# Single-head f1 rows, pair sums in buffers of their own, and half of a weight product moved, in a four-layer GNN kernel

## The chip, the cores and the metric

The kernel runs on one core of a Trainium2 chip. The time is the device time of one execution in microseconds (us). Engines are named as in the profile: PE is TensorE (matmuls; PEld its weight loads), DVE is VectorE, ACT is ScalarE, POOL is GpSimd, SP is SyncE. [...]

## The reference, cut to what matters

A stack of four graph layers on N = 2708 nodes with F = 512 features; each is followed by a residual sum and a layer norm. Only layer 0 (an attention autoencoder with H = 4 heads of D = 128) and the weights of layer 3 are touched by the change:

```python
# layer 0
Xw  = einsum('hnd,hde->hne', Xh, W)
f1  = einsum('hnd,hd->hn', Xw, V[:, 0, :, 0]);  f2 = einsum('hnd,hd->hn', Xw, V[:, 1, :, 0])
sig = sigmoid(f1[:, :, None] + f2[:, None, :])
att = masked_softmax(adj[None] * sig, adj != 0)         # both patterns are adj
Xc  = einsum('hij,hjd->hid', att, Xw)  ->  n x F
Xn  = batchnorm(Xc)
emb = batchnorm(elu(Xn @ Wm.T + bm) + Xn)               # encoder MLP
Y   = einsum('hij,hjd->hid', att, emb by heads)
Yc  = elu(einsum('hnd,hed->hne', Y, W))
out = batchnorm(elu(Yc @ Wd.T + bd) + Yc)               # decoder MLP
x   = layernorm(x + out)
# layer 3
a = (x @ Wq + bq) @ (x @ Wk + bk).T * scale + adj + adj;  x = layernorm(x + softmax(a) @ (x @ Wv + bv))
```

Layer 1 multiplies by the adjacency divided by its column degrees, layer 2 is an edge softmax over all nodes.

## The kernel before

Nodes are cut into 22 blocks of 128 rows (the last has 20); the 2708 columns of the attention matrix into two halves `hf` of HW = 1354; the heads into two pairs `p`. What decides the order of instructions on each engine is the tile scheduler, which places them by the program's order, by `issue_after` and by free buffers: `att.tile(..., tag=..., bufs=n)` takes one of n buffers of that tag, and waits until the readers of the tile that had it are done. An engine runs its instructions in the built order, so one that waits holds up all behind it. Loads go on SP's queue, most stores on POOL's.

`attention_pass` (L423 and on) runs twice, in the encoder on `xw` and in the decoder on `emb`, each time over the four stages (hf, p) = (0,0), (0,1), (1,0), (1,1), each with 22 blocks of source nodes. For a block, `form` (L358 to L405) makes a tile `t` of 128 x 2 x 1354: ACT takes a tanh for each of the pair's heads (L396), of the row `f1b` (the f1 of 1354 target nodes, the same in all partitions) with f2 as bias; DVE adds a constant and multiplies by the block `a` of the adjacency (L404); ACT takes the exponential (L405). Then PE multiplies `t` by the values into six accumulators `po` (L471). `a` comes from `adjT`, or, from the second pair on, from `adj_d`, a copy whose zeros have been made -1e30: in stage p = 0 of the encoder (`prepare`) DVE makes that copy with two instructions on buffers `z` and `a` (L385, L386) and POOL stores it. Five blocks a stage keep their `t` in memory in the encoder and load it again in the decoder, with no `form`.

The row tile `f1b` holds both heads, 128 x 2 x 1354, has two buffers, and is loaded by one transfer on SP at the start of a stage, placed behind the load of `a` that is ninth from the end. For the first stage it comes from `project` (L238 to L270), which makes the rows with PE, writes them to `f1_d` and loads them back.

In the encoder, PE also sums the columns of `t` with a ones matrix (L494, into `psm`): for blocks alone where `prepare` holds, and otherwise for the first four and the last two blocks; else DVE first adds a block's `t` to the one before it, in place in that tile (L488), and PE sums the pair.

At the end of a stage `keep` (L576) copies the six `po` to `ft` (L580, three by DVE and three by ACT), and leaves the scaling by the softmax sums for later. At the end of stage (0,1) it also makes the product of the encoder's weight with beta, `small_product`: four matmuls (L546), a copy of the row by DVE (L549), four matmuls that turn it into a column (L551), and an add into `bias` (L586). The next stage then starts.

Behind the four stages the encoder takes the batch norm's scale, transposes Wq and Wk (L668), scales `enc_w`, and makes the merged weight `mqk` of layer 3 (Wq Wk^T, 16 matmuls at L696, four copies L703, four stores to `mqk_d` at L705), a vector `uq`, and the MLP (L724). After the MLP's first group a small product with the mean corrects the bias. The result is transposed to `emb` (L756).

The decoder pass takes `a` from `adj_d` with three buffers, and its `decode` (L816) copies `po` out with a scale (L825), shifts (L838), turns (L850) and runs the decoder's MLP (L859), much of it spread over the next stage's blocks. After its last stage come the batch scale, and layer 1: a memset of the last rows of `hid_hi` (L966) and a copy of the weight (L976) on DVE, then for each block a normalisation (L983 on ACT, L990 on DVE), a transpose (L996) and the hidden product (L128 in `project_rows`).

Of the kernel before, what the change touches and what calls it, by code (L numbers as in the profile page):

```python
# [8 lines left out]
F32 = mybir.dt.float32  # L9
# [3 lines left out]
AF = mybir.ActivationFunctionType  # L13
ALU = mybir.AluOpType
# [3 lines left out]
P = 128  # L18
# [11 lines left out]
def gnn_stack_kernel(  # L30
# [25 lines left out]
    nc = tc.nc  # L56
# [107 lines left out]
    adj_d = dram.tile([N, N], F32, name="adj_d")  # L164
    mqk_d = dram.tile([C, P, C, P], F32, name="mqk_d")
    qscale = float(1.0 / F**0.5)
    uq = const.tile([P, C], F32, name="uq")
# [3 lines left out]
    with ExitStack() as l0:  # L171
# [40 lines left out]
        def project(att, psum):  # L212
# [33 lines left out]

            stage = att.tile([P, HP, HW], F32, tag="f1b", name="f1_rows", bufs=2)[:, 0, :]
            f1b = att.tile([P, HP, HW], F32, tag="f1b", name="f1b", bufs=2)

# [14 lines left out]
            for ci, (q0, _) in enumerate(HCH[0]):  # L264
                f1_rows(ci, stage[:, q0:])
            nc.sync.dma_start(f1_d[:, h0 : h0 + w], stage[0 : 32 * H : 32, :w])
            spread = nc.sync.dma_start(
                f1b[:, :, :w], f1_d[:HP, h0 : h0 + w].partition_broadcast(P)
            )
            def values_of(jt):  # L270
# [61 lines left out]
        def attention_pass(values, first, att, psum, finish, f1b=None, blocks=(), spread=None, rest=None, taken={}):  # L332
# [5 lines left out]
            def count(hf, jt, att, a=None):  # L338

                h0, w = HSPAN[hf]  # L340
                j0, n = BLOCKS[jt]
                if a is None:
                    a = att.tile([P, HW], F32, tag="a", name="a", bufs=3)
                    nc.sync.dma_start(a[:n, :w], adj_d[j0 : j0 + n, h0 : h0 + w])
                z = att.tile([P, HW], U8, tag="z", name="z", bufs=1)
                nc.vector.tensor_scalar(
                    z[:n, :w],
                    a[:n, :w],
                    -0.5 * BIG,
                    None,  # L350
                    ALU.is_lt,
                    ALU.add,
                    accum_out=zeros[:n, jt, hf : hf + 1],
                )

            def form(hf, p, jt, att, prepare, f1b, tv):
# [6 lines left out]
                else:  # L363
                    a = att.tile([P, HW], F32, tag="a", name="a", bufs=4 if first else 3)

# [28 lines left out]
                for k in range(HP):  # L394
                    h = HP * p + k
                    nc.scalar.activation(  # L396
                        tv[:, k, :],
                        f1b[:n, k, :w],
                        AF.Tanh,
                        bias=f2h[:n, jt, h : h + 1],  # L400
                        scale=0.5,
                    )
# [13 lines left out]
            for hf, (h0, w) in enumerate(HSPAN):  # L416
                for p in range(H // HP):
                    prepare = first and p == 0
                    if f1b is None or not prepare or hf > 0:
                        f1b = att.tile([P, HP, HW], F32, tag="f1b", name="f1b", bufs=2)  # L420

                        with tc.issue_after(loads[-9].ins) if len(loads) > 8 else nullcontext():
                            nc.sync.dma_start(  # L423
                                f1b[:, :, :w],
                                f1_d[HP * p : HP * (p + 1), h0 : h0 + w].partition_broadcast(P),
                            )
                    rb = None if first else spread_sums(att, hf, p)
# [4 lines left out]
                    for place, jt in enumerate(ORDER):  # L432
# [45 lines left out]
                        if not first:  # L478
                            continue

                        if prepare or not ALONE <= place < NT - LAST:
                            whole, m = t, n
                        elif place % 2 == 0:
                            before = t
                            continue
                        else:
                            whole, m = before, P
                            nc.vector.tensor_tensor(  # L488
                                whole[:n, :, :w], whole[:n, :, :w], tv, ALU.add
                            )  # L490
                        for k in range(HP):
                            for r, (q0, qw) in enumerate(SCH[hf]):
# [3 lines left out]
                                    ones32[:m],  # L496
                                    whole[:m, k, q0 + qw - SW : q0 + qw],
                                    start=(place == 0),
# [64 lines left out]
        with (  # L563
# [8 lines left out]
            def keep(hf, p, po, sums):  # L572
# [4 lines left out]
                for k in range(HP):  # L577
                    for q, (q0, qw) in enumerate(HCH[hf]):
# [3 lines left out]
                        )  # L582
                if hf == 0 and p == 1:
                    row = att.tile([P, HW], F32, tag="z", name="row", bufs=1)[:1, :F]
                    ps = small_product(po[0], mlp_w[0], prm_sb[:, B_ENC, :], row)
                    nc.vector.tensor_tensor(bias[:, 0, :], ps, prm_sb[:, MB_ENC, :], ALU.add)  # L586
                sm = [att.tile([P, BW], F32, tag="rs", name="sm") for _ in range(HP)]
# [53 lines left out]
            attention_pass(xw, True, att, psum, keep, f1b, blocks, spread, rest, taken)  # L641
            scale1, mean1 = batch_scale(stats, G_ENC, "bn1")


# [29 lines left out]
        with (  # L674
            tc.tile_pool(name="att_c", bufs=1) as att,
            tc.tile_pool(name="ps_c", bufs=1, space=PSUM) as psum,
        ):

            (enc_w,) = mlp_w
            for c in range(C):
                if c % 2:
# [7 lines left out]
            stats = stats_tile("stats_b", NCH)  # L691
            mqk = emb[:, NT - 3 * C : NT - 2 * C, :]
            for c in range(C):
                ps = psum.tile([P, F], F32, tag="misc", name="ps_m", bufs=2)
                for o in range(C):
                    nc.tensor.matmul(  # L696
                        ps,
                        wqT[:, o, c * P : (c + 1) * P],
                        wkT[:, o, :],
                        start=(o == 0),  # L700
                        stop=(o == C - 1),
                    )
                nc.scalar.activation(mqk[:, c, :], ps, AF.Copy, scale=qscale)  # L703
            for o in range(C):
                nc.gpsimd.dma_start(mqk_d[o], mqk[:, :, o * P : (o + 1) * P])  # L705

            row = emb[:1, NT - 3 * C - 2 : NT - 3 * C, :]
            pu = small_product(
# [7 lines left out]
            for ci, (c0, w) in enumerate(CHUNKS):  # L716
                pss = []
                for o in range(C):
# [12 lines left out]
                    pss.append(ps)  # L731
                    if ci == 0 and o == 0:
                        pm = small_product(
                            psum.tile([P, F], F32, tag="misc", name="ps_mean", bufs=2),
                            enc_w,
                            mean1,
                            row[:, 1, :],
                        )
                        nc.vector.tensor_tensor(bias[:, 0, :], bias[:, 0, :], pm, ALU.subtract)
                        nc.vector.tensor_scalar(  # L740
                            bias[:, 1, :], bias[:, 0, :], 1.0, None, ALU.subtract
                        )
                for o in range(C):
# [25 lines left out]
            links = {}  # L769
            spare = []  # L770

            def centre(pm):
# [34 lines left out]
            def decode(hf, p, po, rb):  # L807
# [45 lines left out]
                def mlp(q, o, st, wide):  # L853
# [4 lines left out]
                    for c in range(C):  # L858
                        nc.tensor.matmul(  # L859
                            ps[:, :qw],  # L860
# [72 lines left out]
                for q in range(HB):  # L933
# [8 lines left out]
                    if q == 0:  # L942
                        centre(po[0])
                    mlp(q, 3, st, True)

            attention_pass(emb, False, att, psum, decode)
# [812 lines left out]
```

## Time and profile before

| what | value |
|---|---|
| median of 3 runs | 3288.74 us (3287.61 to 3291.08) |
| the profiled execution's own time | 3290.97 us |
| span of that execution in the trace | 3289.17 us, mean granted clock 0.991 |
| L404, DVE, 128 x 2708 | 156 times, mean 2975 ns |
| L396, ACT, 128 x 1354 | 312 times, mean 1413 ns |
| L405, ACT, 128 x 2708 | 156 times, mean 2455 ns |
| L471, PE, on `xw` and on `emb` | 415.9 us and 403.1 us in all |

The stages in the trace, with PE's busy time (times from the start of the span):

| stretch (us) | what | PE busy | DVE busy | ACT busy |
|---|---|---|---|---|
| 0 to 37 | values and f1 rows | 28.45 of 37 | 13.75 | 13.35 |
| 37 to 165 | encoder (0,0), `prepare` | 124.76 of 128 | 118.30 | 113.03 |
| 165 to 301 | encoder (0,1) | 131.42 of 136 | 98.46 | 115.32 |
| 301 to 314 | change to column half 1 | 4.13 of 13 | 9.07 | 6.27 |
| 314 to 576 | encoder (1,0), (1,1) | 255.72 of 262 | 218.76 | 213.75 |
| 576 to 636 | weights, start of the MLP | 55.84 of 60 | 48.17 | 35.13 |
| 636 to 910 | rest of the MLP, decoder's first half | 264.16 of 274 | 184.63 | 187.32 |
| 910 to 1207 | decoder's second half | 289.01 of 297 | 228.60 | 196.40 |
| 1207 to 1300 | end of layer 0 | 90.89 of 93 | 72.03 | 49.92 |
| 1300 to 3289 | layers 1 to 3 | 1977.30 of 1989 | 952.79 | 418.03 |

How to read the profile's lines: "L471 MATMUL po<-t,xw" is an instruction of line 471 that writes `po` from `t` and `xw`. In a list of waits, "PE po L471 <- ACT t L405: 23.7, 12, 8.2" says that PE's instruction at L471 waited for ACT's at L405 for 23.7 us in all, 12 times, the longest 8.2. In a timeline, a row has its start, its duration, engine, line, operation, out<-in with shapes and the number of instructions, and in brackets the idle time before it and what ended it. In a table of stretches, a row has the stretch, its length, PE's busy time (x instructions), the granted clock of TensorE (1 is full speed), the share of the DMA engines' time in use and GB/s.

### The profile page before, as it was taken

How to read it: one execution, taken by the hardware profiler on the slowest of the kernel's cores; microseconds unless marked ns; L12 is line 12 of the kernel's file. 1: busy time of each engine (PE TensorE's matmuls, PEld its weight loads, DVE VectorE, ACT ScalarE, POOL GpSimd, SP SyncE). 2: the span in 40 equal slices, each digit the busy share in tenths (PEclk: the TensorE clock that was granted, in tenths of full speed). 3: DMA queues.
4: the chain of work that ended last, by engine and by line, in shares of the span. 5: the costliest groups of instructions: out<-in, count | busy, mean ns of one | idle time of the engine just before them, and what ended most of it. 6: DMA issues, size and time to landing. Idle time of an engine off the chain costs nothing.

```text
span 3289.2 us, 30359 instructions
## 1 busy us (share of the span) xinstructions
PE 3221.7 (98%) x10922; PEld 1722.4 (52%) x10922; DVE 1944.6 (59%) x3144; ACT 1348.5 (41%) x1512; POOL 129.7 (4%) x211
## 2 busy tenths in 40 slices
PE   8998999999999999999999999999999999999999
PEld 5443444454444445885555555554455555555554
DVE  7877977767687596445136666777252452543433
ACT  6887887557877753001133434443020120210211
POOL 1100100000000000000011000000000000000000
PEclk9999999999999999999999999999999999999999
DMA  8855863335555322550034444554211111111100
GB/s 283 305 187 171 302 233 124 106 102 183 185 179 172 134 81 67 144 145 21 0 102 133 122 124 136 148 159 125 68 49 33 44 31 43 40 34 43 36 24 20
DMA packets 172550, 381.45 MB, mean 116 GB/s; under 512 B 20938, under 2 KB 115094, under 8 KB 167982
## 3 DMA queue, kind: packets, MB, share of 16 engines
q1 hardware_dynamic: 156926, 308.16, 30.9%
q0 software_dynamic: 15472, 71.33, 5.8%
q8 instruction: 86, 1.41, 0.2%
q14 instruction: 66, 0.54, 0.1%
HBM read 307.22 MB, written 71.67 MB: 115 GB/s over the span
## 4 chain that ended last, share of the span: by engine, by line
PE 88%; DVE 5%; ACT 2%; DMA 2%; issue 1%; SPq 0%; DVEq 0%; ACTq 0%
PE po L1324 23%; PE po L471 19%; PE ps_s L1203 18%; PE ps_nb L1056 6%; PE ps_wide L1105 4%; PE psm L494 3%; DVE t L404 2%; PE ps_hid L128 2%; PE ps_sup L1501 2%; PE ps_o L1432 2%; PE ps_mlp L724 2%; PE ps_dec L859 2%; DMA a<-adj_d 1%; ACT t L405 1%; ACT t L396 1%
## 5 line engine op out<-in xcount | busy, mean ns | idle before, releaser
L404 DVE SCALAR_TENSOR_TENSOR t<-t,a 128x2708 f32<-128x2708 f32 (+1 forms) x156 | 462.2, 2975 | 124.1 <-ACT t L396 120.1
L396 ACT ACTIVATE t<-f1b,f2h 128x1354 f32<-128x1354 f32 (+1 forms) x312 | 428.3, 1413 | 60.5 <-PE po L471 28.7
L471 PE MATMUL po<-t,xw 128*128 128x452 f32 (+3 forms) x1056 | 415.9, 557 | 14.6 <-ACT t L405 14.6
L405 ACT ACTIVATE t<-t 128x2708 f32<-128x2708 f32 (+1 forms) x156 | 382.6, 2455 | 112.7 <-DVE t L404 112.4
L471 PE MATMUL po<-t,emb 128*128 128x452 f32 (+3 forms) x1056 | 403.1, 550 | 12.3 <-ACT t L405 9.2
L1203 PE MATMUL ps_s<-sup,hT 128*128 128x384 f32 (+1 forms) x1176 | 407.4, 490 | 0.0
L1324 PE MATMUL po<-sup,e 128*128 128x512 f32 x882 | 407.0, 595 | 0.0
L1324 PE MATMUL po<-e,xs 128*128 128x384 f32 (+1 forms) x1176 | 406.0, 489 | 0.0
L1635 DVE SCALAR_TENSOR_TENSOR e<-a_cols,ps_s 128x384 f32<-128x384 f32 (+1 forms) x154 | 85.5, 556 | 451.1 <-PE ps_s L1203 428.2
L471 PEld LDWEIGHTS po<-t,xw 128*128 128x128 f32 (+1 forms) x1056 | 191.5, 193 | 227.4 <-issue 202.0
L1203 PEld LDWEIGHTS ps_s<-sup,hT 128*128 128x128 f32 x1176 | 221.8, 190 | 164.2 <-issue 14.2
L471 PEld LDWEIGHTS po<-t,emb 128*128 128x128 f32 (+1 forms) x1056 | 194.9, 192 | 213.5 <-issue 188.7
L1324 PEld LDWEIGHTS po<-e,xs 128*128 128x128 f32 x1176 | 222.2, 190 | 160.2 <-issue 5.8
L1324 PEld LDWEIGHTS po<-sup,e 128*128 128x128 f32 x882 | 160.4, 190 | 159.3 <-issue 137.1
L1203 PE MATMUL ps_s<-hT 128*128 128x384 f32 (+5 forms) x672 | 211.1, 461 | 0.9 <-ACT sup L1508 0.7
L1302 ACT ACTIVATE e<-e 128x384 f32<-128x384 f32 (+1 forms) x308 | 151.7, 522 | 116.0 <-DVE e L1301 113.3
L1056 PE MATMUL ps_nb<-hid_hi,at 128*128 128x512 f32 x484 | 185.4, 390 | 0.4 <-DVE at L1048 0.4
L1550 ACT ACTIVATE a_cols<-a_cols,neg_big 128x384 f32<-128x384 f32 (+1 forms) x154 | 94.7, 617 | 220.9 <-DMA a_cols<-in_adjT_dram 183.3
L1056 PE MATMUL ps_nb<-hid_lo,at 128*128 128x512 f32 x462 | 179.9, 389 | 0.0
L108 ACT ACTIVATE ln_rstd<-ln_rstd 128x1 f32<-128x1 f32 (+1 forms) x88 | 17.2, 201 | 391.7 <-DVE ln_rstd L107 391.2
L1301 DVE TENSOR_TENSOR e<-e,nmax 128x384 f32<-128x384 f32 (+1 forms) x308 | 163.1, 552 | 23.3 <-ACT nmax L1294 23.3
L1203 PEld LDWEIGHTS ps_s<-hT 128*128 128x128 f32 x672 | 123.1, 190 | 89.5 <-issue 19.4
(252 smaller groups left out, 3325.8 us busy)
## 6 DMA issues: line engine op xcount, KB each, us to landing
a<-adj_d SPq DMA_DIRECT2D x110, 677.0 KB
a_cols<-in_adjT_dram SPq DMA_DIRECT2D x378, 192.0 KB
a<-in_adjT_dram SPq DMA_DIRECT2D x42, 677.0 KB
adj_d<-a POOLq DMA_DIRECT2D x42, 677.0 KB, 5.5
raw<-in_adjT_dram SPq DMA_DIRECT2D x105, 256.0 KB
kept<-t POOLq DMA_DIRECT2D x16, 1354.0 KB, 6.8
t<-kept SPq DMA_DIRECT2D x16, 1354.0 KB
a_cols<-in_adjT_dram SPq DMA_DIRECT2D x63, 202.0 KB
```

The lines of the kernel that those rows point to most:

```text
L396: nc.scalar.activation(tv[:, k, :], f1b[:n, k, :w], AF.Tanh, bias=f2h[:n, jt, h : h + 1], scale=0.5,)
L404: step = nc.vector.scalar_tensor_tensor(tv, tv, GUARD, ab, ALU.add, ALU.mult)
L405: nc.scalar.activation(tv, tv, AF.Exp, scale=0.5)
L471: nc.tensor.matmul(po[HB * k + q][:, :qw], values[r : r + n, jt, h * P : (h + 1) * P], t[r : r + n, k, q0 : q0 + qw], start=(place == 0), ...
L494: nc.tensor.matmul(sums[k][32 * r : 32 * r + 32, :SW], ones32[:m], whole[:m, k, q0 + qw - SW : q0 + qw], start=(place == 0), stop=(place = ...
L1056: nc.tensor.matmul(pos[it][:n], at, half[:, jt, :], start=(jt == 0 and k == 0), stop=(jt == NT - 1),)
L1105: nc.tensor.matmul(ps[:, :width], w(c, o), xt(c), start=(c == 0), stop=(c == C - 1),)
L1203: nc.tensor.matmul(ps[:, b * P : w], keys[:, c, j0 : j0 + P], st["q"][:, c, b * P :], start=(c == 0), stop=(c == C - 1),)
L1301: nc.vector.tensor_tensor(e, e, st["nmax"][:, :w], ALU.add)
L1302: nc.scalar.activation(e, e, AF.Exp)
L1324: nc.tensor.matmul(out, lhsT, rhs, start=(k == 0), stop=(k == NT - 1))
L1550: nc.scalar.activation(a, a, AF.Identity, bias=neg_big[: a.shape[0]], scale=1.0e30)
```

## The change

1. `f1b` becomes one tile a head (128 x 1354) with three buffers instead of two of twice the size. The first head's row is loaded as before on SP; the second head's on ACT's queue in the encoder and on POOL's in the decoder. At the start, the two rows are two transfers.
2. `a` has four buffers in the decoder too.
3. A pair's sum goes, one add a head, into two tiles of 128 x 1354 of their own (tags `z` and `pair`). Only the pair with the 20-row block still adds in place.
4. `keep` no longer makes the product with beta. The encoder makes one with the batch norm's shift instead, and the product with the mean goes.
5. Of `mqk` only rows 0 and 1 of four are made in the encoder. The transposed Wk and half of the transposed Wq are stored to memory, loaded again into two `t` tiles at the end of the decoder, and the other eight matmuls run there, after the decoder's last MLP matmul; ACT copies their result and POOL stores it.

```diff
-            stage = att.tile([P, HP, HW], F32, tag="f1b", name="f1_rows", bufs=2)[:, 0, :]
-            f1b = att.tile([P, HP, HW], F32, tag="f1b", name="f1b", bufs=2)
+            stage, *f1b = [
+                att.tile([P, HW], F32, tag="f1b", name=name, bufs=HP + 1)
+                for name in ["f1_rows"] + ["f1b"] * HP
+            ]
...
-            spread = nc.sync.dma_start(
-                f1b[:, :, :w], f1_d[:HP, h0 : h0 + w].partition_broadcast(P)
-            )
+            for k in range(HP):
+                spread = nc.sync.dma_start(
+                    f1b[k][:, :w], f1_d[k, h0 : h0 + w].partition_broadcast(P)
+                )
...
-                    a = att.tile([P, HW], F32, tag="a", name="a", bufs=4 if first else 3)
+                    a = att.tile([P, HW], F32, tag="a", name="a", bufs=4)
...
-                        f1b[:n, k, :w],
+                        f1b[k][:n, :w],
...
-                        f1b = att.tile([P, HP, HW], F32, tag="f1b", name="f1b", bufs=2)
-                        with tc.issue_after(loads[-9].ins) if len(loads) > 8 else nullcontext():
-                            nc.sync.dma_start(
-                                f1b[:, :, :w],
-                                f1_d[HP * p : HP * (p + 1), h0 : h0 + w].partition_broadcast(P),
-                            )
+                        early = (
+                            tc.issue_after(loads[-9].ins) if len(loads) > 8 else nullcontext()
+                        )
+                        f1b = [
+                            att.tile([P, HW], F32, tag="f1b", name="f1b", bufs=HP + 1)
+                            for k in range(HP)
+                        ]
+                        f1 = f1_d[HP * p : HP * (p + 1), h0 : h0 + w].partition_broadcast(P)
+                        with early:
+                            nc.sync.dma_start(f1b[0][:, :w], f1[:, 0, :])
+                        queue = nc.scalar if first else nc.gpsimd
+                        queue.dma_start(f1b[1][:, :w], f1[:, 1, :])
...
                         if prepare or not ALONE <= place < NT - LAST:
-                            whole, m = t, n
+                            whole, m = [t[:, k, :] for k in range(HP)], n
                         elif place % 2 == 0:
                             before = t
                             continue
+                        elif n < P:
+                            whole, m = [before[:, k, :] for k in range(HP)], P
+                            nc.vector.tensor_tensor(
+                                before[:n, :, :w], before[:n, :, :w], tv, ALU.add
+                            )
                         else:
-                            whole, m = before, P
-                            nc.vector.tensor_tensor(
-                                whole[:n, :, :w], whole[:n, :, :w], tv, ALU.add
-                            )
+                            whole, m = [], P
+                            for k, tag in enumerate(("z", "pair")):
+                                both = att.tile([P, HW], F32, tag=tag, name="pair", bufs=1)
+                                nc.vector.tensor_tensor(
+                                    both[:, :w], before[:, k, :w], tv[:, k, :], ALU.add
+                                )
+                                whole.append(both)
...
-                if hf == 0 and p == 1:
-                    row = att.tile([P, HW], F32, tag="z", name="row", bufs=1)[:1, :F]
-                    ps = small_product(po[0], mlp_w[0], prm_sb[:, B_ENC, :], row)
-                    nc.vector.tensor_tensor(bias[:, 0, :], ps, prm_sb[:, MB_ENC, :], ALU.add)
...
             scale1, mean1 = batch_scale(stats, G_ENC, "bn1")
+            shift1 = batch_shift(scale1, mean1, B_ENC, "bn1")
...
+            merged(0)
...
+            pm = small_product(
+                psum.tile([P, F], F32, tag="misc", name="ps_shift", bufs=2),
+                enc_w,
+                shift1,
+                row[:, 1, :],
+            )
+            nc.vector.tensor_tensor(bias[:, 0, :], pm, prm_sb[:, MB_ENC, :], ALU.add)
+            nc.vector.tensor_scalar(bias[:, 1, :], bias[:, 0, :], 1.0, None, ALU.subtract)
...
+            nc.gpsimd.dma_start(wkT_d, wkT)
+            nc.gpsimd.dma_start(wqT_d, wqT[:, :, half * P :])
+            merged(1)
             for o in range(C):
-                nc.gpsimd.dma_start(mqk_d[o], mqk[:, :, o * P : (o + 1) * P])
-
-            row = emb[:1, NT - 3 * C - 2 : NT - 3 * C, :]
+                nc.gpsimd.dma_start(
+                    mqk_d[o][:, :half, :], mqk[:, :half, o * P : (o + 1) * P]
+                )
...
-                    if ci == 0 and o == 0:
-                        pm = small_product(
-                            psum.tile([P, F], F32, tag="misc", name="ps_mean", bufs=2),
-                            enc_w,
-                            mean1,
-                            row[:, 1, :],
-                        )
-                        nc.vector.tensor_tensor(bias[:, 0, :], bias[:, 0, :], pm, ALU.subtract)
...
+                nc.sync.dma_start(wk_again, wkT_d)
+                nc.sync.dma_start(wq_again, wqT_d)
+                with tc.issue_after(last_dec[0].ins):
+                    for c in range(half):
+                        for o in range(C):
+                            nc.tensor.matmul(
+                                po[1 + c],
+                                wq_again[:, o, c * P : (c + 1) * P],
+                                wk_again[:, o, :],
+                                start=(o == 0),
+                                stop=(o == C - 1),
+                            )
+                for c in range(half):
+                    nc.scalar.activation(mqk[:, c, :], po[1 + c], AF.Copy, scale=qscale)
+                    nc.gpsimd.dma_start(
+                        mqk_d[:, :, half + c, :].rearrange("o p i -> p o i"),
+                        mqk[:, c, :].rearrange("p (o i) -> p o i", o=C),
+                    )
```

Here `merged(c)` (L701 to L711 after) is the old loop over L696 for one c: four matmuls into `ps_m` and ACT's copy to `mqk`.

## Prediction

> **What bounds the kernel now.** First the busy times of the page:
>
> ```profile
> PE 3221.7 (98%) x10922; PEld 1722.4 (52%) x10922; DVE 1944.6 (59%) x3144; ACT 1348.5 (41%) x1512; POOL 129.7 (4%) x211
> ```
>
> TensorE (PE) is busy all but 67.5 us of the span. So a change is worth the PE work it takes out, the PE idle time it closes, and the matmul time that a lowered clock costs. Next, who ended PE's waits (total us, times, longest):
>
> ```profile
> PE po L471 <- ACT t L405: 23.7, 12, 8.2
> PE tp_out L996 <- DVE ot L990: 7.5, 1, 7.5
> PE pxw L275 <- DVE f2h L288: 5.2, 1, 5.2
> PE psm L494 <- DVE t L488: 3.7, 3, 1.4
> PE po L471 <- DVE ot L825: 3.0, 1, 3.0
> ```
>
> Nearly all of it lies in layer 0, which ends near 1300 us: in the attention passes (L471, L494), at their start (L275) and at their end (L996). Layers 1 to 3 are full, and the built instruction order of the changed kernel equals the old one there on every engine. Third, PE at the change from column half 0 to half 1:
>
> ```profile
> 299.32 1.35 PE L494 MATMUL psm<-t,ones 128*32 128x340 f32 x16
> 300.49 3.59 PE L546 MATMUL po<-enc_w,prm_sb 128*1 128x512 f32 x8
> 304.86 1.05 PE L551 MATMUL po<-ones,row 1*128 1x1 f32 x8 [0.77 <-DVE row L549]
> 314.14 6.29 PE L471 MATMUL po<-t,xw 128*128 128x452 f32 x12 [8.24 <-ACT t L405]
> ```
>
> and DVE there:
>
> ```profile
> 304.12 0.68 DVE L549 COPY row<-po 1x512 f32<-1x512 f32 x1 [2.70 <-PE po L546]
> 305.94 0.16 DVE L586 TENSOR_TENSOR enc_bias<-po,prm_sb 128x4 f32<-128x4 f32 x1 [1.14 <-PE po L551]
> 306.02 0.87 DVE L385 TENSOR_SCALAR z<-a 128x1354 f32<-128x1354 f32 x1
> ```
>
> The small product holds PE, then holds DVE in its row, and only then DVE prepares the next block (L385, L386, L404), ACT exponentiates it, and PE goes on. Fourth, stretches with PE's busy time and, after it, the granted clock:
>
> ```profile
> 276.00:283.00 7.00, 6.61 (x14) 0.76 0.72 238
> 306.00:314.00 8.00, 0.00 (x0) 0.56 0.54 151
> 314.00:320.00 6.00, 5.86 (x12) 0.74 0.96 324
> 803.00:811.00 8.00, 8.00 (x15) 0.65 0.84 285
> 1210.00:1220.00 10.00, 10.00 (x25) 0.76 0.38 138
> ```
>
> After each gap PE also works at a lower clock: 7 us at 0.76 lose 1.7 us, 6 at 0.74 lose 1.6, 8 at 0.65 lose 2.8, 10 at 0.76 lose 2.4.
>
> **The change, part by part** (us; minus is a gain; against the profiled execution, 3290.97, span 3289.17).
>
> (a) Start: the f1 rows come as two transfers. PE's 5.16 at 40.24 ends a chain in which DVE's L385 of the third block stands ahead of the first block's L404 and waits 3.37 for its a until 35.67; in the built order L385 stands behind. L404, now at 36.45, then waits only for the tanh of both heads. The joint transfer ended ACT's wait at 33.14; with head 0 earlier, the second head's tanh is over near 34.8. Gain 36.45 − 34.8, about −1.5; bounds 0 (the last byte sets it) and −3.4 (the wait).
>
> (b) Pair sums in their own buffers. The in-place add (L488) must wait until PE has read the first block, and holds L404 of later blocks behind it:
>
> ```profile
> 267.98 2.98 DVE L488 TENSOR_TENSOR t<-t 128x2708 f32<-128x2708 f32 x1 [4.33 <-PE po L471]
> ```
>
> Behind that stand PE's waits 0.47 and 2.69 (257.03, 276.39); half 1 repeats them and adds 0.88 (481.24). With the clock after them (1.7 at 276; 7 us at 0.81 at 550, 1.3) this is 4.9 + 5.3 = 10.2. The 1.41 at 238.23 and 511.62 belong to the 20-row block, which still adds in place. New waits are weaker: a pair buffer must be free of the previous pair's L494, which stands ahead of the next blocks on PE. DVE issues two adds of 1354 columns for one of 2708 (2.98), no more work. ACT becomes second: 22 blocks at two tanh (1.41) and one exp (2.45) are 116, against PE's 126 from 174.44 to 300.67. I take two thirds, −7; bounds 0 and −10.2.
>
> (c) The switch. PE loses 314.14 − 300.49 = 13.65 there and 1.6 of clock. In the built order DVE prepares two blocks (z, a, z, a, two L404) ahead of its copies L580. Replayed with the durations above: last old L404 ends 288.76, the two z/a pairs (2 × 2.44) 293.7, L404 296.7, exp 299.1, second L404 299.6, third copy 301.4; PE, free at 300.67, goes on at 301.4. That leaves under 1 of the 13.65: −13; bounds −8 (a row 5 late, see d) and −15.2. The product is not gone: one with the shift replaces the one with the mean (L546/L551 ps_mean, 3.6 + 1.0), net nothing in the encoder.
>
> (d) The price: with three row buffers, the second head's row takes the slot of the first head's old row, so it is issued only after that head's last tanh: on ACT's queue in the first pass, on POOL's in the second. Behind the waiting tanh on ACT stand the exp of the last old block, the next tanh, and the copies of po, for which PE waits. Between issue and use ACT has a tanh or two and one or two exp, 5.3 to 6.5 us with DVE's L404. A transfer of this size:
>
> ```profile
> adj_d<-a POOLq DMA_DIRECT2D x42, 677.0 KB, 5.5
> ```
>
> So it just fits; at 8.4 (twice the size, 24.70 to 33.14) it would be 2 to 3 late, mostly inside ACT's waits for PE (1.74 at 172.51). I take +1 in all; bounds 0 and +8. [...]
>
> (e) Encoder. Half of L696 leaves (16 of 32 records, 13.97 in all): −7.0. PE's wait 1.36 at 607.53 goes too. New: L703 of the first half stands behind a tanh that waits for its f1 row (ACT's table load waited until 592.60), and the second half waits for its bank: +0.3 to +2.6. DVE, full from 595 to 631, then lets PE wait at the transposes L756: +1 to +3. Sum −4; bounds −8 and +1.
>
> (f) Fourth a buffer in the second pass. DVE waits there for a (3.52, 2.49, 3.96; 34.0 in all), behind which PE waits 12.2 (0.46, 0.43, 1.24, 5.69, 0.68, 3.03, 0.20, 0.46) and loses 2.8 at 803 and some 3 at 905 of clock: 18. A load may now start one block earlier (about 5). But po is still copied out (L825 x6, 3.66) before PE goes on, and L404 of the second new block stays ahead of that. I take −7; bounds −1 and −16.
>
> (g) End of layer 0. The eight products moved from (e), 7.0, fill the 7.53 before L996, and the 2.4 of clock goes. But in the built order DVE's memset of hid_hi, ahead of the weight copy L976, waits for the store of the new mqk. ACT's second copy comes after four L983 (1206.94 + 2.64 + 0.57 = 1210.2), a 256 KB store takes 4.4 (mqk_d, page), memset and copy 0.48 + 1.16: L128 starts near 1216.2. Two blocks (2 × 3.43) end near 1223; before, the second ended at 1219.8. That is +3.2, and a lower clock after this 5 us gap some 2 more: +5; bounds −2.9 (the store lands in cover) and +8. So moving the products gains little.
>
> Sum: −1.5 − 7 − 13 + 1 − 4 − 7 + 5 = −26.5: 3264.5 for the profiled execution, which lies 2.2 above the median 3288.74. **Forecast 3262.**
>
> [...]
>
> **Rivals.**
> - Slower: (d) decides. Six switches, each late by the landing time less 5.5, with 1.7 of clock. Without (d) the sum is −27.5; it is lost when landing reaches 5.5 + 27.5/6 − 1.7 = 8.4, and a measurable loss (+6.6) needs 9.5. The slowest row, a at 25.12, took 10.45: 6 × 6.65 = 40, so 3301. Against it: in 162 to 166 the queues were idle. For it: 424 to 438 they were full. 6%.
> - The changes mostly cancel, since (f) and (b) stay bound by ACT and the end costs 8: −13 + 8 + 1 − 3 = −7 or less: 3282 to 3295 counts as no change (0.2%, 6.6 us, is what a measurement of this kernel can tell). 7%.
> - Only the switch works as told: −13 − 4 + 5 + 1 − 3 = −14: 3275. 22%.
> - All gaps close and the end fills: −1.5 − 9 − 15 − 7 − 12 − 1 = −45: 3243. 13%.
> - The forecast, 3262 within about 9: 52%.
>
> Faster 0.52 + 0.22 + 0.13 = 0.87, same 0.07, slower 0.06. The range reaches into the neighbours: 3242 to 3281.
>
> **What would show it.** (c) right: no L546 before 314 and L471 within 2 us of the last L494 there. (b): no DVE add waits for PE but the 20-row ones. (d): ACT's tanh waits for f1b in single us, not 5. (e): L696's group has 16 records before the MLP. (f): DVE's waits for a well under 34.0. (g): a gap ahead of L128 ended by a DVE copy behind a store. I am wrong if rows land near 10 us, or if the waits of (f) are PE's own release of t.

## The result, and the profile after

The changed kernel takes 3277.83 us (median of 6, 3272.79 to 3280.94) against 3289.46 (6 runs) before: ratio 0.9966, interval 0.9956 to 0.9976. It is faster, by 11.6 us, where 27 were forecast. The time lies inside the range (3242 to 3281), near its slow end; the gain is some 15 short of the forecast. Three more series on other occasions gave 9.3, 10.3 and 11.5 less than the kernel before them.

The profiled execution took 3276.90, its span 3275.1. Lines have moved: L404 is L410 now, L405 L411, L396 L402, L471 L484, L488 L502 (in place) and L510 (separate), L494 L517, L580 L603, L825 L851, L346 L352, L976 L1034, L996 L1054. First the page's busy times, and then who ended PE's waits (total, times, longest):

```profile
PE 3213.4 (98%) x10906; PEld 1721.9 (53%) x10906; DVE 1946.1 (59%) x3158; ACT 1346.6 (41%) x1512; POOL 135.6 (4%) x219
```

```profile
PE po L484 <- ACT t L411: 24.4, 14, 5.7
...
PE ps_hid L128 <- DVE w_sb L1034: 3.9, 1, 3.9
PE pxw L281 <- DVE f2h L294: 2.8, 1, 2.8
PE psm L517 <- DVE t L502: 2.8, 2, 1.4
PE po L484 <- DVE ot L851: 2.5, 1, 2.5
```

The waits for the exponential were 23.7 in 12 times and are 24.4 in 14, although the largest of the old ones, 8.24 at the change of column half, has gone. So new ones have come. A table by stage finds them. Each column is the time from one mark on PE to the next, the first from the start of the span: the last group of values (L281) that waited at the start; Wq's first transpose; the encoder's last group of transposes to `emb`; the first MLP matmul of the decoder's last part (L885); layer 1's first product.

| kernel | to L281 | passes of the encoder | end of the encoder | decoder | end of layer 0 |
|---|---|---|---|---|---|
| before | 40.24 | 534.09 | 128.38 | 442.11 | 152.65 |
| changed | 37.86 | 512.25 | 123.81 | 451.87 | 157.58 |
| difference | -2.4 | -21.8 | -4.6 | +9.8 | +4.9 |
| forecast | -1.5 (a) | -19 (b, c, d) | -4 (e) | -7 (f) | +5 (g) |

The sum of the differences is -14.1, the difference of the two spans; from layer 1 on nothing changed. Four of five columns agree with the forecast within 3. The decoder has the wrong sign, and is off by 17. How far can one trace be trusted here? In the 15 traces below whose code is the same up to Wq's first transpose, that transpose comes at 547.3 to 553.4 (574.3 before), so the first two columns together are good to some 3 either way. The decoder's column is 451.3 to 451.9 in the eight traces that have the changed decoder, so its loss is well clear of this.

At the change of column half, the place of the largest gain, DVE (first) and PE (second) now read:

```profile
285.94 5.86 DVE L410 SCALAR_TENSOR_TENSOR t<-t,a 128x2708 f32<-128x2708 f32 x2
291.72 2.35 DVE L603 COPY ft<-po 128x452 f32<-128x452 f32 x4
```

```profile
287.52 4.82 PE L484 MATMUL po<-t,xw 128*128 128x452 f32 x12
292.26 1.35 PE L517 MATMUL psm<-t,ones 128*32 128x340 f32 x16
293.55 4.82 PE L484 MATMUL po<-t,xw 128*128 128x452 f32 x12
```

Both L410 for the new half are done before DVE copies `po` out, and PE goes on without a gap. The granted clock is 1.00 there. That is step (c) as it was replayed.

In the decoder, at the change to its last stage, a gap is new. DVE, then SP's issues, then PE:

```profile
1001.42 5.87 DVE L410 SCALAR_TENSOR_TENSOR t<-t,a 128x2708 f32<-128x2708 f32 x2 [3.92 <-ACT t L402]
1012.79 1.56 DVE L352 TENSOR_SCALAR_CACHE_REDUCE z<-a 128x1354 uint8<-128x1354 f32 x1 [5.50 <-DMA a<-adj_d]
...
1014.28 5.86 DVE L410 SCALAR_TENSOR_TENSOR t<-t,a 128x2708 f32<-128x2708 f32 x2
```

```profile
1004.43 0.32 SPq L375 DMA_DIRECT2D a<-adj_d  x1
...
1007.32 0.32 SPq L375 DMA_DIRECT2D a<-adj_d  x1
```

```profile
1021.49 4.79 PE L484 MATMUL po<-t,emb 128*128 128x452 f32 x12 [2.47 <-DVE ot L851]
```

L352 counts the zeros of a block of `a`. SP could issue the loads of the next two blocks only at 1004.43 and 1007.32, each when one of the two L410 had freed its buffer, and DVE stands 5.50 in front of the count until one has landed. Behind it are two L410, two blocks of work, and behind those the copies L851, for which PE then waits 2.47. Before, PE had no gap at this place. The two L404 there waited only for ACT, with no count ahead of them:

```profile
1034.22 5.87 DVE L404 SCALAR_TENSOR_TENSOR t<-t,a 128x2708 f32<-128x2708 f32 x2 [4.62 <-ACT t L396]
```

This is one of several new gaps. In the whole of the decoder's column, PE waited 12.2 before and waits 22.9 now (before first):

```profile
PE po L471 <- ACT t L405: 9.2, 7, 5.7
PE po L471 <- DVE ot L825: 3.0, 1, 3.0
```

```profile
PE po L484 <- ACT t L411: 20.4, 10, 5.7
PE po L484 <- DVE ot L851: 2.5, 1, 2.5
```

The others, of 2.00 to 4.90, were not followed to a single instruction of DVE.

### The profile page after: what moved, and what is told of

Its sections match the earlier page's. It is cut to its first block, busy times and chain, and to the rows that moved or that the text cites. A ratio compares the mean times of both kernels' runs of the same rounds, so it can differ in the third digit from the quotient of the medians.

```text
span 3275.1 us, 30408 instructions
## 1 busy us (share of the span) xinstructions
PE 3213.4 (98%) x10906; PEld 1721.9 (53%) x10906; DVE 1946.1 (59%) x3158; ACT 1346.6 (41%) x1512; POOL 135.6 (4%) x219
## 3 DMA queue, kind: packets, MB, share of 16 engines
q8 instruction: 86, 1.41, 0.2%
## 4 chain that ended last, share of the span: by engine, by line
PE 77%; issue 12%; DVE 4%; ACT 3%; DMA 2%; POOL 1%; SPq 0%; POOLq 0%; DVEq 0%; ACTq 0%
PE po L1382 23%; PE ps_s L1261 17%; PE po L484 10%; PE ps_nb L1114 6%; PE ps_wide L1163 4%; PE ps_hid L128 2%; PE ps_sup L1559 2%; PE ps_o L1490 2%; DVE t L410 2%; PE ps_dec L885 2%; ACT t L411 2%; PE ps_mlp L760 1%; ACT t L402 1%; PE psm L517 1%; DMA a<-adj_d 1%
## 5 line engine op out<-in xcount | busy, mean ns | idle before, releaser
L410 DVE SCALAR_TENSOR_TENSOR t<-t,a 128x2708 f32<-128x2708 f32 (+1 forms) x156 | 461.5, 2975 | 128.5 <-ACT t L402 124.6
L402 ACT ACTIVATE t<-f1b,f2h 128x1354 f32<-128x1354 f32 (+1 forms) x312 | 427.5, 1413 | 53.0 <-PE po L484 23.7
L411 ACT ACTIVATE t<-t 128x2708 f32<-128x2708 f32 (+1 forms) x156 | 382.2, 2454 | 110.6 <-DVE t L410 110.4
L484 PE MATMUL po<-t,emb 128*128 128x452 f32 (+3 forms) x1056 | 402.4, 550 | 22.9 <-ACT t L411 20.4
L484 PE MATMUL po<-t,xw 128*128 128x452 f32 (+3 forms) x1056 | 411.7, 554 | 4.1 <-ACT t L411 4.0
L484 PEld LDWEIGHTS po<-t,emb 128*128 128x128 f32 (+1 forms) x1056 | 195.0, 192 | 223.1 <-issue 192.5
L484 PEld LDWEIGHTS po<-t,xw 128*128 128x128 f32 (+1 forms) x1056 | 190.2, 191 | 214.2 <-issue 198.3
```

Source lines behind the costliest of these rows:

```text
L402: nc.scalar.activation(tv[:, k, :], f1b[k][:n, :w], AF.Tanh, bias=f2h[:n, jt, h : h + 1], scale=0.5,)
L410: step = nc.vector.scalar_tensor_tensor(tv, tv, GUARD, ab, ALU.add, ALU.mult)
L411: nc.scalar.activation(tv, tv, AF.Exp, scale=0.5)
L484: nc.tensor.matmul(po[HB * k + q][:, :qw], values[r : r + n, jt, h * P : (h + 1) * P], t[r : r + n, k, q0 : q0 + qw], start=(place == 0), ...
```

## The experiments

Times are medians in us; "under before" is against runs of the kernel before on the same occasion, "under changed" against the changed kernel there.

**1. The decoder as it was** (the new branch stands beside `if first:`; the encoder keeps its single rows and four buffers; `count`'s own `a` has three buffers again too).

```diff
+                        else:
+                            both = att.tile([P, HP, HW], F32, tag="f1b", name="f1b", bufs=2)
+                            with early:
+                                nc.sync.dma_start(
+                                    both[:, :, :w],
+                                    f1_d[HP * p : HP * (p + 1), h0 : h0 + w].partition_broadcast(P),
+                                )
+                            f1b = [both[:, k, :] for k in range(HP)]
...
-                    a = att.tile([P, HW], F32, tag="a", name="a", bufs=4)
+                    a = att.tile([P, HW], F32, tag="a", name="a", bufs=4 if first else 3)
```

> The changed kernel with the decoder's pass as it was: both heads' f1 rows in one tile of two buffers, loaded by one transfer on SP, and three buffers for a; its built order in the decoder is that of the kernel before. From the last transpose of the encoder to the first of the decoder's last MLP matmuls the changed kernel took 9.8 us longer than the kernel before. Theory A (the fourth buffer of a and the order built for it cost it) and theory B (the second head's row on POOL's queue costs it) both expect these 9.8 back: some 21 under the kernel before, and PE's waits for the exponential in the decoder near 12 in all instead of 23. Theory C (the decoder is only shifted against the DMA queues by an encoder that ends earlier, and loses wherever its loads then fall) expects no gain: some 12 under the kernel before.

Measured 3262.57, 27.8 under before (ratio 0.9918, interval 0.9905 to 0.9932). The decoder's column is 442.00, the old 442.11. Theory C falls: with the same shifted start the old decoder loses nothing.

> The decoder's pass as it was, again, now beside the changed kernel: theory A expects 10 us less than the changed kernel; the first time it was 28 under the kernel before, which would be 16 less.

Measured 3266.41, 22.5 under before (0.9927, 0.9915 to 0.9940) and 12.1 under changed; decoder 438.74. So the decoder's two edits lose 10 to 13 by the decoder's column, and 12 by the times of this occasion.

**2. Three buffers for `a`, rows of single heads kept** (the last two lines of that diff, and the same in `count`).

> The changed kernel with three buffers for a in the decoder, the f1 rows of single heads kept. Theory A: 8 to 10 us faster than the changed kernel, some 20 under the kernel before; DVE no longer waits in a count (L352) for a load ahead of a ready L410 at the change to the last stage (5.50 us at 1012.79 in the changed kernel). Theory B and theory C: within 2 us of the changed kernel, some 12 under the kernel before.

Measured 3267.66, 22.7 under before (0.9938, 0.9925 to 0.9950); decoder 442.24. The whole loss of the decoder goes with the fourth buffer. At the same change of stage, DVE has no count ahead of L410:

```profile
996.06 5.87 DVE L410 SCALAR_TENSOR_TENSOR t<-t,a 128x2708 f32<-128x2708 f32 x2 [3.92 <-ACT t L402]
1006.55 5.87 DVE L410 SCALAR_TENSOR_TENSOR t<-t,a 128x2708 f32<-128x2708 f32 x2 [4.62 <-ACT t L402]
1012.33 3.65 DVE L851 SCALAR_TENSOR_TENSOR ot<-po,bn_scale,rb 128x452 f32<-128x452 f32 x6
```

**3. Four buffers, but each count behind its own L410.**

```diff
-                if not first and p == (jt in KEPT[0]):
-                    count(hf, jt, att, a)
...
                 nc.scalar.activation(tv, tv, AF.Exp, scale=0.5)
+                if not first and p == (jt in KEPT[0]):
+                    with tc.issue_after(step.ins):
+                        count(hf, jt, att, a)
```

> The changed kernel, but the count of a block's zeros (L352) is placed behind the block's own L410 instead of ahead of it, so that DVE does not stand in a count whose load is late while an older block's L410 is ready. Four buffers of a as in the changed kernel. Theory A in its sharper form (it is the counts ahead of ready L410s that hold DVE): 10 us or more faster than the changed kernel, 22 or more under the kernel before, DVE's waits of counts for a (34.8 in all) near 0 and no such wait at L410 in their place. Theory D (the loads themselves are late, whatever stands ahead): within 3 us of the changed kernel, and the waits for a move from the count to L410.

Measured 3267.18, 23.2 under before (0.9932, 0.9918 to 0.9946); decoder 440.95. With four buffers and the counts out of the way, the loss is gone as well. In the decoder's stretch DVE waited for `a` in the kernel before and, no less, in the changed kernel (first and second line). Here these waits fall to nothing, and what is left on DVE, then on ACT, then on PE of this kernel (its L407 is L410, L399 is L402, L408 is L411) is:

```profile
DVE z L346 <- DMA a<-adj_d: 31.4, 15, 4.0
DVE z L352 <- DMA a<-adj_d: 34.2, 15, 5.5
```

```profile
DVE t L407 <- ACT t L399: 107.4, 33, 5.7
```

```profile
ACT t L408 <- DVE t L407: 56.5, 45, 4.0
ACT t L399 <- PE po L484: 31.1, 17, 6.9
```

```profile
PE po L484 <- ACT t L408: 8.4, 4, 6.4
PE po L484 <- DVE ot L851: 5.8, 2, 4.9
```

PE still waits 14.2, against 12.2 before, with no load late; its longest wait, 5.69 before (at 802.57, the decoder's first change of stage), is 6.36 here, at the same change. So the 31.4 that DVE waited for `a` in the decoder before look like slack (experiment 5 tests this with three buffers). By the waits that are left, what PE waits behind is ACT and DVE taking turns (tanh, L410, exponential), and `t` buffers that PE itself had not freed. Theory D falls.

**4. The second head's row on SP in the decoder.**

```diff
-                        queue = nc.scalar if first else nc.gpsimd
+                        queue = nc.scalar if first else nc.sync
```

> The changed kernel with the second head's row in the decoder on SP's queue instead of POOL's; the built order of every other engine is the same. Theory A: within 2 us of the changed kernel, since ACT waited for that row only 1.03 us; if anything worse, since the row now stands in the queue of the loads of a. Theory B: 5 to 10 us faster, 17 to 21 under the kernel before.

Measured 3271.19, 19.2 under before (0.9943, 0.9930 to 0.9955): more than theory A allowed, and inside the 17 to 21 of theory B. One sentence of that expectation is wrong: the built order is the same in the decoder proper, but at the end of the encoder, where the decoder's first blocks lie beside the MLP, DVE's order differs. It was run again beside the changed kernel:

> The changed kernel again, for comparison with the three others on the same chip: 10 to 12 us under the kernel before.

> The second head's row in the decoder on SP's queue again, now beside the changed kernel on one chip: the first time it stood 19 us under the kernel before where the changed kernel stood 9 to 12, though its decoder was only 2.3 us shorter in the trace. If POOL's queue matters (theory B), 5 us or more faster than the changed kernel here too; if not, the two intervals overlap and it is within 3 us.

Measured 3278.52 and 3272.36: 6.2 under changed, and no run of the one reached into those of the other. By stage it is 3.2 at the end of the encoder (120.88 for 124.03) and 2.5 in the decoder (449.30 for 451.78). Then the queue was changed where the counts do no harm:

> The changed kernel, for comparison on the same chip: 9 to 12 us under the kernel before.

> Three buffers for a in the decoder, and the second head's row on SP's queue there. If POOL's queue itself costs 6 us, this is some 16 us faster than the changed kernel (28 under the kernel before); if the counts were the cause there too, it is like a_three, 10 to 12 faster than the changed kernel (some 22 under the kernel before).

> Four buffers, the counts behind their own L410, and the second head's row in the decoder on SP's queue. If POOL's queue itself costs 6 us: 16 or more faster than the changed kernel. If only the counts' place does: like count_late, some 11 faster. A cost of the late counts with four buffers would show as less.

Measured 3277.03, 3262.83 and 3264.42. The two are 14.2 and 12.6 under changed (25.8 and 24.2 under before; ratios 0.9927 and 0.9928, intervals 0.9915 to 0.9940 and 0.9914 to 0.9941), between the two predictions. The stages say more: their decoders, 441.37 and 441.18, are like those of a_three and count_late with POOL (442.24, 440.95), so POOL's queue costs the decoder nothing there. Why the same move shortens the decoder by 2.5 where the counts stand ahead (449.30, and 449.58 the first time) is not shown. The end of the encoder is again 2.1 and 3.7 shorter on SP (121.10 for 123.21, 119.63 for 123.37). ACT waits some 3 us for the first row there on either queue (2.9 to 3.1), so it is not the row's arrival. DVE has fewer counts ahead of the MLP's work until about 600 (four for six, and with late counts three for four); whether that is the cause was not isolated and stays open.

**5. Late counts with three buffers.** Experiments 1 and 3 together.

> The decoder's pass as it was (three buffers of a, one tile for both rows), with the count of zeros (L352) behind the block's own L410. If DVE's waits for a were slack, as four buffers with late counts showed (no such wait left, and still 14.1 us of PE's waits, against 12.2 before), this is within 2 us of dec_old_2. If they did hold PE, it is 5 us or more faster. If three buffers that come free 1.57 us later delay the loads, it is 3 us or more slower, with DVE waiting for a at L410.

Measured 3262.56, 26.3 under before (0.9921, 0.9908 to 0.9935), 3.9 under dec_old_2, but the runs of the two overlap (3259.00 to 3265.33 and 3259.03 to 3268.70), and its decoder, 440.72, lies between the 438.74 and 442.00 of the two runs of the old one. Not told apart; a large gain or loss is excluded. Its trace settles what the waits for `a` were worth with three buffers, too: in the decoder DVE waited 29.9 for `a` in dec_old and waits 1.9 here, and PE's waits are the same, 12.4 there and 12.6 here:

```profile
PE po L493 <- ACT t L408: 6.8, 2, 6.4
PE po L493 <- DVE ot L860: 5.8, 2, 4.9
```

**6. The pair's sum in place again** (step b alone undone): `elif n < P:` becomes `elif True:`.

> The changed kernel itself, for comparison with the three others on the same chip: some 12 us under the kernel before.

> The changed kernel with the pair's sum added in place again (term b undone alone). The forecast's step: 7 us slower than the changed kernel (0 to 10.2), all of it before Wq's first transpose, with DVE's add again waiting for PE in the row of each pair. Rival: the gain came from the f1 rows and the shorter switch, and the sums give under 2 us.

Measured 3278.35 for the changed kernel and 3286.59: 8.2 slower, as forecast (7). All of it lies in the encoder's passes (520.54 for 509.65 and 512.25; Wq's first transpose comes at 558.4, outside the 547.3 to 553.4). The old pattern is back, DVE's add behind PE and PE's gap after it:

```profile
265.84 2.98 DVE L502 TENSOR_TENSOR t<-t 128x2708 f32<-128x2708 f32 x1 [4.33 <-PE po L484]
```

```profile
274.25 4.22 PE L484 MATMUL po<-t,xw 128*128 128x452 f32 x6 [2.69 <-ACT t L411]
```

**7. The product with beta back in `keep`** (step c alone undone).

```diff
+                if hf == 0 and p == 1:
+                    row = att.tile([P, HW], F32, tag="z", name="row", bufs=1)[:1, :F]
+                    ps = small_product(po[0], mlp_w[0], prm_sb[:, B_ENC, :], row)
...
-            pm = small_product(..., enc_w, shift1, row[:, 1, :])
...
+                        pm = small_product(..., enc_w, mean1, row[:, 1, :])
```

> The changed kernel with the product with beta back in keep, at the change of column half, and the product with the mean back in the encoder (term c undone alone). The forecast's step: 13 us slower than the changed kernel (8 to 15.2), before Wq's first transpose, and PE's gap of some 8 us ahead of the first L484 of half 1. Rival: with separate sums and earlier rows the switch is short anyway, under 5 us.

Measured 3293.16: 14.8 slower than the changed kernel, and slower than the kernel before (ratio 1.0016, 1.0007 to 1.0025). The product and the gap behind it return, with the old 0.77 and 8.24:

```profile
296.33 3.59 PE L569 MATMUL po<-enc_w,prm_sb 128*1 128x512 f32 x8
300.70 1.05 PE L574 MATMUL po<-ones,row 1*128 1x1 f32 x8 [0.77 <-DVE row L572]
309.98 2.63 PE L484 MATMUL po<-t,xw 128*128 128x452 f32 x3 [8.24 <-ACT t L411]
```

Some 2.8 of it is at the encoder's end (126.81 for 124.04), where the product with the mean now stands beside the MLP; the forecast had that at nothing.

**8. All of mqk in the encoder** (steps e and g undone): `for c in range(1, C): merged(c)` in place of `merged(1)`, and no products behind the decoder.

> The changed kernel with all four rows of mqk made and stored in the encoder, and nothing of it at the end of the decoder (terms e and g undone). The forecast's steps give e + g = -4 + 5, so undoing both gains some 1 us; by the trace of the changed kernel, 7.0 more in the encoder and 4.9 less from the decoder's last MLP matmuls to layer 1, so some 2 slower. Rival: the move of the eight products is worth its 7.0, and this is 7 us slower; or the wait for the late store costs more than the end's gap did, and this is 3 or more faster. In the decoder no change (within 2).

Measured 3279.30, 1.0 slower than the changed kernel, with overlapping runs: the same. By stage, 5.7 more at the end of the encoder (129.71) and 5.1 less at the end of layer 0 (152.79). The move of eight matmuls brings nothing, as forecast.

**9. Without the late stores.**

```diff
+                nc.gpsimd.dma_start(
+                    mqk_d[o][:, half:, :], mqk[:, :half, o * P : (o + 1) * P]
+                )
...
-                    nc.gpsimd.dma_start(
-                        mqk_d[:, :, half + c, :].rearrange("o p i -> p o i"),
-                        mqk[:, c, :].rearrange("p (o i) -> p o i", o=C),
-                    )
```

> The changed kernel without the two late stores of mqk: rows 2 and 3 of mqk are not stored, and rows 0 and 1 are stored in their place in the encoder, so layer 3 runs with a wrong weight of the same size. The eight products and ACT's copies stay. If the weight copy (L1034) and with it L128 are held by the late store, as forecast, PE's gap of 3.94 ahead of L128 shrinks below 2 and the low clock behind it (0.73) goes: 4 to 6 us faster than the changed kernel. If they are held by DVE's other work at that place, within 1.5 us of it.

Measured 3271.33, 5.7 under changed; the end of layer 0 takes 151.79 for 157.58. PE there in the changed kernel, and in this one:

```profile
1182.39 7.03 PE L990 MATMUL po<-wk_again,wq_again 128*128 128x512 f32 x16
1191.15 1.09 PE L1054 MATMUL tp_out<-ident,ot 128*128 128x128 f32 x8 [1.74 <-ACT wq_again L998]
1196.19 9.70 PE L128 MATMUL ps_hid<-w_sb,ot 128*128 128x512 f32 x16 [3.94 <-DVE w_sb L1034]
```

```profile
1193.09 1.09 PE L1053 MATMUL tp_out<-ident,ot 128*128 128x128 f32 x8 [1.74 <-ACT wq_again L1001]
1194.89 5.42 PE L128 MATMUL ps_hid<-w_sb,ot 128*128 128x512 f32 x12 [0.71 <-DVE w_sb L1033]
```

The products fill the old gap of 7.53, and the wait for the weight copy makes one of 3.94. The granted clock after it (fourth column: PE busy, then the clock), changed kernel first:

```profile
1191.00:1196.00 5.00, 1.09 (x8) 0.86 0.24 75
1196.00:1206.00 10.00, 9.81 (x19) 0.73 0.70 240
```

```profile
1191.00:1201.00 10.00, 7.54 (x23) 1.00 0.69 209
```

So step (g) was right for its reason, the late store, and not only in its sum. DVE does not stand idle for the store, though: it has other work ahead of the memset, which starts 12.2 after the first of the late products with the store and 9.0 without. How much of this is the store's landing, and how much the order built round it, is not told apart.

## Why the prediction was wrong, step by step

- **(a) Start**, -1.5: measured -2.4. The first block's L410 no longer stands behind the third block's L391 and starts at 34.07, where L404 started at 36.45. Right, and a little larger.
- **(b) Pair sums**, -7: undone alone they cost 8.2. Right; only the in-place adds of the 20-row block still wait for PE. Two adds take 2 × 1.56 for the one of 2.98, which the step put at no more work. Not all gaps closed: PE still waits 2.37 (at 504.12) in the changed kernel.
- **(c) The switch**, -13: undone alone it costs 14.8, and the traces show the 13.65 (the product and the gap behind it) and the low clock gone. Right; 2.8 of the 14.8 is a term that was set at nothing, the product with the mean.
- **(d) Rows**, +1, and the rival that ended slower: the trace has the landing of the four rows on POOL's queue: 4.3 to 6.5 us, median 5.3, against the 5.5 assumed and the 9.5 of the rival. Between the encoder's stages ACT never waited for a row; it waited 1.03 in the decoder, and some 3 at the decoder's start (2.95 to 3.15 in the three later traces of this kernel). The rival did not occur.
- **(e) Encoder's end**, -4: -4.6. Right. One reading in it does not hold: the profile puts the wait of ACT's table load until 592.60 down to the load of `rb`, not of the f1 row.
- **(g) End of layer 0**, +5: +4.9, by the mechanism named. Right, with two sizes off that cancel: the late stores landed in 2.7 each, not 4.4, and the two blocks behind the gap took 9.7, where 6.9 and 2 of clock were set.
- **(f) The fourth buffer**, -7 with bounds of -1 and -16: +9.8. **This step failed**, and it alone makes up the shortfall: with the decoder as it was, the same kernel takes 3262.57 and 3266.41, against a forecast of 3262. Two things in it were wrong. Its premise was that DVE's waits for `a` (34.0 in the step, 31.4 of them in this stretch) are what PE waits behind. With late counts those waits are gone and PE's are not: 14.2 with four buffers, 12.6 with three, against 12.2 before. And its bounds took for granted that another buffer can only help. In fact DVE runs in the built order (before 1012.79 it stood 5.50 in a count, with two L410 behind it), and the order built with four buffers puts the counts of later blocks, whose loads cannot start earlier than a buffer comes free, ahead of L410s that are ready. The sign that the prediction set for this step, waits for `a` well under 34.0, did not come: they are 34.8 in all. The trace of before could not show the new order; the built order of the changed kernel could, and the prediction does not use it for the place of the counts. It named the right thing to watch ("the waits of (f) are PE's own release of t"), and did not let it into the range. That the time lies inside the range all the same is luck: no case in it has a decoder that loses.

The rival with the nearest time, 3275, where only the switch works, is not what happened: the pair sums work too, and the decoder loses.

What is shown: the fourth buffer makes the loss (experiment 2), and it goes too when the counts stand behind their L410 (3). That a single gap comes from one such count is read from the trace at one place; the late counts also moved other instructions. What stays open: the other new gaps one by one, and why the row on SP makes the encoder's end 2 to 4 shorter, and the decoder too where the counts stand ahead.

The fastest versions run keep three buffers in the decoder (the old decoder, with early or late counts, or rows of single heads) with the rows on SP. They took 3262.56 to 3266.41, 22 to 28 under the kernel before and 12 to 16 under the changed one where that ran beside them. Four buffers with late counts and the row on SP, 3264.42, cannot be told apart from them.

## What to carry to other kernels

A wait on an engine that is not the bottleneck is worth what stands behind it, not its length (here the 31.4 that DVE waited for `a` went, and PE waited 14.2 where it had waited 12.2): replay what that engine does next before a buffer is bought for it. A further buffer also changes the order that a scheduler builds (here a count that waited 5.50 came ahead of two L410); look in that order for instructions that wait for a late load and now stand ahead of work that is ready. Put work that nobody waits for behind the work of the same tile (here a count; with it there, the decoder's column went from 451.87 to 440.95).

## What the runs showed of the hardware

The granted clock did not fall by the length of a gap alone. In one execution of the changed kernel, it was 0.76 in the stretch with a gap of 1.41, and 1.00 in another with a gap of 1.41 and in one with 2.47:

```profile
235.00:242.00 7.00, 6.55 (x26) 0.76 0.32 101
489.00:496.00 7.00, 6.18 (x29) 1.00 0.31 98
1021.00:1029.00 8.00, 7.51 (x20) 1.00 0.90 340
```

So a gap may cost some 1.7 us more (7 at 0.76) or nothing, and step (b)'s price of a low clock for each gap was a price for the execution profiled. It may be part of why six runs of the changed kernel lie 8 us apart: the fastest has a mean granted clock of 0.995 and the three slowest 0.993, of which 0.002 of 3277 would be 6.6. That was not tested.
